# The last block of a three-layer kernel: work in halves on two engines, centred weights, and fewer small operations

## The chip, the cores and the metric

The kernel runs on one core of a Trainium2 chip. A core has a matrix engine (TensorE, "PE" in the profile, with its weight loads as "PEld"), a vector engine (VectorE, "DVE"), a scalar engine for activations (ScalarE, "ACT"), a general engine (GpSimd, "POOL") and a queue engine that issues most DMA transfers (SyncE, "SP"). Each engine works through its own list of instructions in order and waits on semaphores for the others. The metric is the device time of one execution in microseconds (us); shown is the median of several runs.

## What is computed

The input is x, (4, 128, 64, 64) in float32: 4 batches of 4096 tokens with 128 channels. Three layers follow each other, all in float32:

```python
# layer 0: attention over all tokens, 64 inner channels, no scale
q, k, v = wq @ xf, wk @ xf, wv @ xf
x = x + wo @ (softmax(k^T q) @ v)
# layer 1, attention: causal, over LayerNorm(t), scale 128**-0.5
t = t + softmax(causal(q k^T * scale)) @ v
# layer 1, recurrence
Wx = LayerNorm(t) @ W.T
Wx = (Wx - mean) * rsqrt(var + 1e-5) * gamma + beta   # mean, var over all 4*4096 tokens
y = 0
for each token: y = sigmoid(Wx[token] + y @ V.T)
t = t + ys
```

What matters here is the seam between the two parts of layer 1: the mean and variance over all tokens of `Wx` have to be complete before the first step of the recurrence, so the last block of the causal attention stands between the two.

## The kernel before, in words

`fast_path` does all of it, with the whole activation in SBUF: `xs` has 128 partitions and, for each of the 4 batches (B), 4096 columns in 8 blocks (NB) of 512 (BLK), each block being 4 pieces (TPB) of 128 tokens. An exact but slow `general_path` stands behind a flag at the end; it isn't entered for these inputs.

The attention of both layers is one list of `items`. An item is a pair of key tiles for one block of 512 queries: `scores` (lines 824 to 863) computes products into PSUM and takes their exponential on ACT, `sums` adds up denominators on DVE, `values` (885 to 923) multiplies the probabilities with the values two items later and accumulates in `acc`. When a block's last item is done, `values` copies `acc` to SBUF as `agg` (line 921 in layer 1, one ACT copy of 512 columns).

What follows for a block of layer 1 is `finish1` (721 to 800), a generator whose steps are drawn into the loop at due slots: `folded` turns the denominators (for the last block by a small product, `den_ps`, with `own` from it at line 595), `first` multiplies `agg` with the value weights (`projected`, `o_ps`, line 614), scales and adds the residual (`joined`, line 624), writes the result to DRAM and takes the LayerNorm's moments (`moments`, 629 to 640; the power -0.5 on POOL at line 638). `norm` sharpens the reciprocal root by one Newton step (`newton`, 460 to 468) and normalises four pieces on DVE (line 645). `second` transposes the normalised block; `third` multiplies it with the recurrence's weights `wf` (line 769), takes statistics on DVE (772) and copies the product to `xs` on ACT (779 or 782).

All blocks but the last transpose by DVE and DMA and lie beside other items' work. For the last block (`final`, batch 3, block 7) nothing is left to lie beside it. It transposes on PE into one PSUM tile (653), copies that on DVE (654), and `warm` fills PE with products whose result nobody reads, 9, 1 and 6 of them (line 730; two passes each).

After it, lines 1035 to 1046 make one `scale` and one `shift` per channel from the statistics of all 32 blocks: `ends` holds the aggregate of the first 31 in three columns and the last block's in six more. `rsqrt` (456 to 459) is the power on POOL and a Newton step. `shift_half` adds `v_half`, a product of V with 0.5 made early (`form_half`, 486 to 489), because the recurrence starts from 0.5.

The recurrence (1064 to 1087) doesn't walk all 4096 tokens in turn: each batch is cut into 256 chunks of 16 tokens that run side by side, each started 11 steps early. So there are 27 steps for each of 4 batches: a product with V on PE (`y_ps`, 1077), `z = Wx * scale + y_ps` on DVE (1079), and a sigmoid with `shift` as its bias on ACT (1082). The very first one (1074) takes `scale` and `shift_half` straight into the sigmoid. At the end `residual` transposes the states, adds the layer's input and writes the output.

Tile, the layer under the kernel, sets all semaphores and lays out the order of each engine's instructions by a plan of its own, program order being the priority. `tc.keep_in_program_order` pins an instruction. [...]

```python
            if not final:
                yield 1, norm
            yield 2, second
            yield 1 if final else 6 if g < 2 or g == NB - 1 else 4, third
```

Of the kernel before, what the change touches and what calls it, by code (L numbers as in the profile page):

```python
# [349 lines left out]
def fast_path(  # L350
# [98 lines left out]
    ends = const.tile([P, 9], F32, name="ends")  # L449
# [3 lines left out]
    v_half = const.tile([P, 1], F32, name="v_half")  # L453
    spare = const.tile([P, 1], F32, name="spare")

    def rsqrt(y, var, z):

        nc.gpsimd.tensor_tensor(y, var, mhalf[:, : y.shape[-1]], ALU.pow)
        newton(y, var, z)

    def newton(y, var, z, pinned=False):
        ins = nc.vector.tensor_tensor(z, y, y, ALU.mult)
        if pinned:

            tc.keep_in_program_order(ins)
        nc.vector.tensor_tensor(z, z, var, ALU.mult)
        nc.vector.tensor_scalar(z, z, -0.5, 1.5, ALU.mult, ALU.add)
        nc.vector.tensor_tensor(y, y, z, ALU.mult)

    with tc.tile_pool(name="batch", bufs=1) as batch, tc.tile_pool(name="rows", bufs=2) as rowp, tc.tile_pool(  # L470
        name="prob", bufs=4
# [6 lines left out]
        def misc(name):  # L478
            return ps_m.tile([P, BLK], F32, tag="m", name=name)
# [95 lines left out]
        def rows1(b, g):  # L575
# [3 lines left out]
            nc.scalar.copy(r, ps)  # L579
            bs[b].next.append(r)  # L580

        def folded(den, by_pe):
# [45 lines left out]
        def moments(b, g):  # L628

            st = stat.tile([P, TPB, nc.vector.BN_STATS_DIM], F32, tag="st", name="ln_st")  # L630
            mv = stat.tile([P, TPB, nc.vector.BN_AGGR_DIM], F32, tag="mv", name="ln_mv")
            for j in range(TPB):
                nc.vector.bn_stats(st[:, j], xs[:, b, ds(g * BLK + j * P, P)])  # L633
                nc.vector.bn_aggr(mv[:, j], st[:, j])
            var = stat.tile([P, TPB], F32, tag="var", name="ln_var")
            nc.vector.tensor_scalar(var, mv[:, :, 1], LN_EPS, None, ALU.add)  # L636
            y = stat.tile([P, TPB], F32, tag="rstd", name="ln_rstd")
            nc.gpsimd.tensor_tensor(y, var, mhalf, ALU.pow)  # L638
            return mv, var, y

        def normed(b, g, dst, mv, var, y, pinned=True):

            newton(y, var, stat.tile([P, TPB], F32, tag="z", name="ln_z"), pinned)
            for j in range(TPB):
                nc.vector.tensor_scalar(  # L645
                    dst[:, j], xs[:, b, ds(g * BLK + j * P, P)], mv[:, j, 0:1], y[:, j : j + 1], ALU.subtract, ALU.mult
                )

        def transposed(src, dst, name, engine):

            ps = misc(name)
            for j in range(TPB):
                nc.tensor.transpose(ps[:, ts(j, P)], src[:, j], ident)
            engine(dst, ps)
# [66 lines left out]
        def finish1(b, g):  # L721
# [4 lines left out]
            def warm(n, rhs):  # L726

                ps = ps_s.tile([P, 2 * BLK], F32, tag="s", name="warm_ps")
                for _ in range(n):
                    nc.tensor.matmul(ps[:, : BLK // 2].rearrange("p (a c) -> p a c", c=P) if len(rhs.shape) == 3 else ps[:, : BLK // 2], lhsT=ident, rhs=rhs, start=True, stop=True)  # L730

            def first():
                if final:
# [11 lines left out]
                mem["of"] = moments(b, g)  # L745

            def norm():
                normed(b, g, mem["xh"], *mem["of"], not final)
# [18 lines left out]
            def third():  # L767
                wp = misc("wx_ps")
                nc.tensor.matmul(wp, lhsT=wf, rhs=mem["xhT"], start=True, stop=True)  # L769
                if b == B - 1 and g == NB - 1:  # L770
                    in_range(True)
                nc.vector.bn_stats(ends[:, 3:] if final else stats[:, b * NB + g], wp)  # L772
                if b == B - 1 and g == NB - 2:
                    ahead()
                    in_range(False)

                to = xs[:, b, ts(g, BLK)]
                if final:
                    nc.scalar.copy(to.rearrange("p (s c) -> p s c", c=CPB), wp.rearrange("p (c s) -> p s c", s=STEPS))
                    warm(6, to[:, : BLK // 2])  # L780
                else:
                    nc.scalar.copy(  # L782
                        to.rearrange("p (s j q u) -> p s j q u", q=Q, j=TPB, s=STEPS),
                        wp.rearrange("p (q j u s) -> p s j q u", q=Q, j=TPB, s=STEPS),
                    )

            by_pe = final or g < 2

# [96 lines left out]
        def values(it):  # L885
# [24 lines left out]
            if it.last:  # L910
                if it.layer == 0:

                    if it.g == 0:
                        bt.xhT = batch.tile([P, N], F32, tag="xhT", name="xhT")
                    bt.agg = bt.xhT[:, ts(it.g, BLK)]
                    half = wk.tile([P, 2, BLK], F32, tag="half", name="half")
                    nc.scalar.copy(half, bt.acc)
                    nc.vector.tensor_tensor(bt.agg, half[:, 0], half[:, 1], ALU.add)
                else:
                    bt.agg = wk.tile([P, BLK], F32, tag="agg", name="agg")  # L920
                    nc.scalar.copy(bt.agg, bt.acc[:, 0])
# [102 lines left out]
    with tc.tile_pool(name="xr", bufs=1) as xrp, tc.tile_pool(name="y", bufs=2) as yp, tc.tile_pool(  # L1024
# [9 lines left out]

        mv = xrp.tile([P, nc.vector.BN_AGGR_DIM], F32, name="mv")
        nc.vector.bn_aggr(mv, ends)
        scale = xrp.tile([P, 1], F32, name="scale")
        var = xrp.tile([P, 1], F32, name="var")
# [7 lines left out]
        nc.vector.tensor_tensor(shift_half, shift, v_half, ALU.add)  # L1046
# [135 lines left out]
```

## Time and profile before

| what | us |
|---|---|
| median of 3 runs (lowest to highest) | 2064.52 (2064.33 to 2066.47) |
| the profiled execution, its own time | 2065.22 |
| span of its instructions | 2063.5 |
| PE busy in the span | 2046.0 |
| DVE busy | 1492.2 |
| ACT busy | 990.1 |
| POOL busy | 135.5 |
| mean granted TensorE clock | 0.999 of full speed |

The page also cuts the span into 40 equal slices of 51.6 us; each digit is an engine's busy share of a slice in tenths:

```profile
PE   9999999999999999999999999999999999999998
PEld 3333354444333345444333335544433334544456
DVE  4899867455889986644679987754588998764578
ACT  5666633323666643333466663332366664333365
POOL 1000011000000001000000001100000001100000
PEclk9999999999999999999999999999999999999999
```

PE is full in every slice but the last. The seam between attention and recurrence lies in the last slice but one, around 1974 to 1988 us, and is too short to be seen at this grain; it has to be looked up in the timeline. Durations below are those of this one execution, whose time stands 0.70 us above the median.

### The profile page before, as it was taken

Reading aid. Unit: us, or ns where it says so; the run is one execution under the profiler, and the core shown is the slowest. Engines: PE = TensorE matmul, PEld = TensorE weight load, DVE = VectorE, ACT = ScalarE, POOL = GpSimd, SP = SyncE. Lnnn points to the kernel's source line nnn. Section 1 sums busy time; section 2 is a strip of 40 time slices with the busy share of each in tenths; the row PEclk is TensorE's granted clock in tenths of the full one; section 3 lists DMA queues with packets and bytes.
Section 4 is the critical chain, followed back from the end, with each engine's and each line's share of the span. In section 5 each row is a group of like instructions: output and inputs, shape, how many; then the busy total and the mean of one; then the engine's idle time right before and its main releaser. Section 6 shows DMA issues by size and latency. Waiting matters only on the chain.

```text
span 2063.5 us, 30798 instructions
## 1 busy us (share of the span) xinstructions
PE 2046.0 (99%) x11716; PEld 896.4 (43%) x11716; DVE 1492.2 (72%) x2865; ACT 990.1 (48%) x1071; POOL 135.5 (7%) x221
## 2 busy tenths in 40 slices
PE   9999999999999999999999999999999999999998
PEld 3333354444333345444333335544433334544456
DVE  4899867455889986644679987754588998764578
ACT  5666633323666643333466663332366664333365
POOL 1000011000000001000000001100000001100000
PEclk9999999999999999999999999999999999999999
DMA  4111012220100111231011101222000111110044
GB/s 113 43 23 23 12 42 51 69 67 16 57 8 17 23 28 46 62 77 41 17 43 22 23 12 42 47 67 72 16 17 5 19 23 28 41 43 25 16 169 165
DMA packets 207148, 89.03 MB, mean 43 GB/s; under 512 B 140960, under 2 KB 189600, under 8 KB 205968
## 3 DMA queue, kind: packets, MB, share of 16 engines
q1 hardware_dynamic: 205984, 86.42, 16.4%
q8 instruction: 94, 1.54, 0.3%
q14 instruction: 62, 0.51, 0.1%
q0 software_dynamic: 288, 0.39, 0.1%
q10 hardware_dynamic: 720, 0.16, 0.0%
HBM read 45.84 MB, written 36.89 MB: 40 GB/s over the span
## 4 chain that ended last, share of the span: by engine, by line
PE 97%; DVE 1%; issue 1%; DMA 0%; ACT 0%; POOL 0%; DVEq 0%; POOLq 0%; ACTq 0%
PE s_ps L844 22%; PE acc L903 22%; PE s_ps L835 22%; PE acc L895 21%; PE o_ps L614 3%; PE y_ps L1077 2%; PE r_ps L577 1%; PE wx_ps L769 1%; PE kr_ps L520 1%; PE v_ps L532 1%; DVE xr L1098 1%; PE warm_ps L484 0%; DMA swap<-kr 0%; ACT p L849 0%; DMA out_x<-xr 0%
## 5 line engine op out<-in xcount | busy, mean ns | idle before, releaser
L875 DVE TENSOR_TENSOR dsum<-dsum,p 128x1024 f32<-128x1024 f32 x676 | 826.0, 1222 | 430.2 <-ACT p L851 312.3
L849 ACT ACTIVATE p<-s_ps,nshift 128x1024 f32<-128x1024 f32 x512 | 569.6, 1117 | 315.0 <-PE s_ps L835 304.4
L851 ACT ACTIVATE p<-s_ps 128x1024 f32<-128x1024 f32 (+2 forms) x288 | 274.5, 953 | 605.5 <-PE s_ps L844 603.2
L895 PE MATMUL acc<-p,v 64*64 64x512 f32 x4096 | 529.2, 590 | 0.0
L835 PE MATMUL s_ps<-swap,kr 64*64 64x512 f32 x2048 | 524.1, 591 | 2.5 <-ACT p L849 1.6
L835 PE MATMUL s_ps<-kr 64*64 64x512 f32 x2048 | 524.1, 591 | 0.0
L844 PE MATMUL s_ps<-rows,xhT 128*128 128x512 f32 (+3 forms) x1152 | 502.9, 559 | 0.0
L903 PE MATMUL acc<-p,xh 128*128 128x512 f32 (+3 forms) x1152 | 500.8, 557 | 0.0
L903 PEld LDWEIGHTS acc<-p,xh 128*128 128x128 f32 x1152 | 216.2, 190 | 244.3 <-issue 233.5
L844 PEld LDWEIGHTS s_ps<-rows,xhT 128*128 128x128 f32 x1152 | 213.8, 190 | 242.4 <-issue 204.6
L895 PEld LDWEIGHTS acc<-p,v 64*64 64x64 f32 x4096 | 155.5, 133 | 281.7 <-issue 269.8
L835 PEld LDWEIGHTS s_ps<-swap,kr 64*64 64x64 f32 x2048 | 139.6, 133 | 141.1 <-issue 125.2
L835 PEld LDWEIGHTS s_ps<-kr 64*64 64x64 f32 x2048 | 139.7, 133 | 138.0 <-issue 133.8
L638 POOL TENSOR_TENSOR ln_rstd<-ln_var,mhalf 128x4 f32<-128x4 f32 x64 | 89.4, 1397 | 1102.1 <-DVE ln_var L636 1102.1
L883 DVE TENSOR_TENSOR dsum<-dsum,p 128x256 f32<-128x256 f32 (+1 forms) x120 | 54.9, 493 | 66.8 <-POOL p L855 66.8
L624 DVE SCALAR_TENSOR_TENSOR xs<-o_ps,recs,xs 128x128 f32<-128x128 f32 x256 | 75.0, 341 | 3.8 <-PE o_ps L614 0.5
L645 DVE TENSOR_SCALAR xh<-xs,ln_mv,ln_rstd 128x128 f32<-128x128 f32 x256 | 71.4, 342 | 2.2
L855 POOL TENSOR_SCALAR_AFFINE_SELECT p<-p 128x128 f32<-128x128 f32 x128 | 35.4, 300 | 466.6 <-ACT p L851 451.8
L633 DVE BATCH_NORM_STATS2 ln_st<-xs 128x6 f32<-128x128 f32 x256 | 63.3, 270 | 0.0
L782 ACT COPY xs<-wx_ps 128x512 f32<-128x512 f32 x31 | 18.1, 585 | 74.6 <-DVE stats L772 68.4
L873 DVE COPY dsum<-p 128x1024 f32<-128x1024 f32 x60 | 41.0, 684 | 12.1 <-ACT p L851 7.8
L1079 DVE SCALAR_TENSOR_TENSOR z<-xs,scale,y_ps 128x256 f32<-128x256 f32 x104 | 46.8, 480 | 2.9 <-PE y_ps L1077 1.7
(138 smaller groups left out, 984.6 us busy)
## 6 DMA issues: line engine op xcount, KB each, us to landing
xs<-in_xT SPq DMA_DIRECT2D x32, 256.0 KB, 2.9
by_r<-sqT SPq DMA_DIRECT2D x128, 64.0 KB, 2.2
xhT<-by_r SPq DMA_DIRECT2D x128, 64.0 KB, 2.0
x<-xs SPq DMA_DIRECT2D x32, 256.0 KB, 2.3
xr<-x SPq DMA_DIRECT2D x8, 1024.0 KB, 12.6
out_x<-xr SPq DMA_DIRECT2D x16, 512.0 KB, 4.7
by_c<-sqT SPq DMA_DIRECT2D x124, 64.0 KB, 1.8
xhT<-by_c SPq DMA_DIRECT2D x31, 256.0 KB, 2.6
```

Of the source, the lines that this page charges most:

```text
L614: nc.tensor.matmul(op[:, ts(j, P)], lhsT=agg[:, ts(j, P)], rhs=wv1 if layer else wo2, start=True, stop=True)
L624: nc.vector.scalar_tensor_tensor(t, in0=op[:, ts(j, P)], scalar=rec[:, j : j + 1], in1=t, op0=ALU.mult, op1=ALU.add)
L633: nc.vector.bn_stats(st[:, j], xs[:, b, ds(g * BLK + j * P, P)])
L638: nc.gpsimd.tensor_tensor(y, var, mhalf, ALU.pow)
L645: nc.vector.tensor_scalar(dst[:, j], xs[:, b, ds(g * BLK + j * P, P)], mv[:, j, 0:1], y[:, j : j + 1], ALU.subtract, ALU.mult)
L835: nc.tensor.matmul(ps[c * M : c * M + M, off : off + n], lhsT=bs[it.b].kr[part, h, ds(t % (NT // 2) * P + c * M, M)], rhs=rows[h], start=True,
L844: nc.tensor.matmul(ps[:, off : off + n], lhsT=lhsT, rhs=rhs, start=True, stop=True)
L849: nc.scalar.activation(it.p[:, :off], ps[:, :off], AF.Exp, bias=nshift)
L851: nc.scalar.activation(it.p[:, :off], ps[:, :off], AF.Exp, scale=float(P) ** -0.5)
L875: nc.vector.tensor_tensor(flat, flat, it.p, ALU.add)
L895: nc.tensor.matmul(bt.acc[h * M : h * M + M, r], lhsT=bt.v[part, t % (NT // 2), t // (NT // 2)], rhs=it.p[part, o : o + n], start=it.first ...
L903: nc.tensor.matmul(bt.acc[:, 0, q0:], lhsT=bt.xh[:, t], rhs=it.p[:, o : o + n], start=it.first and h == 0, stop=it.last and h == 1,)
```

## The change

- `values`: for the very last block the copy of `acc` is cut in two, columns 0 to 255 on ACT and 256 to 511 on DVE, and `own` in `folded` is ordered behind the DVE half.
- `newton` takes `half = -0.5 * var`, made beside the power, and does three operations in place of four, the last two fused.
- `normed` for the last block: pieces 0 and 2 on DVE, 1 and 3 on ACT, multiplied by the reciprocal root only. The mean isn't subtracted; instead the last block's product uses `wfc`, weights multiplied from the left by `ident - 1/128`, made early in `form_half`.
- `second` for the last block: the four transposes go into two PSUM tiles, copied by DVE and ACT. The one warming product there is gone.
- `third` for the last block: two products of 256 columns in two tiles, with statistics on DVE and a copy on ACT for each; `ends` grows from 9 to 15 columns. Six warming products follow, now pinned to program order.
- Scale and shift: fused operations, with `beta_half` (beta plus V times 0.5) made early in place of `v_half`; `shift` comes after `shift_half`.

```diff
+    center = const.tile([P, P], F32, name="center")
+    nc.vector.tensor_scalar(center, ident, -1.0 / P, None, ALU.add)
+    wfc = const.tile([P, P], F32, name="wfc")
...
-    def newton(y, var, z, pinned=False):
+    def newton(y, half, z, pinned=False):
+
         ins = nc.vector.tensor_tensor(z, y, y, ALU.mult)
...
-        nc.vector.tensor_tensor(z, z, var, ALU.mult)
-        nc.vector.tensor_scalar(z, z, -0.5, 1.5, ALU.mult, ALU.add)
-        nc.vector.tensor_tensor(y, y, z, ALU.mult)
+        nc.vector.tensor_tensor(z, z, half, ALU.mult)
+        nc.vector.scalar_tensor_tensor(y, in0=z, scalar=1.5, in1=y, op0=ALU.add, op1=ALU.mult)
...
-            nc.vector.tensor_copy(v_half, hp[:, 0:1])
+            nc.vector.tensor_tensor(beta_half, hp[:, 0:1], beta, ALU.add)
+            cp = misc("c_ps")
+            nc.tensor.matmul(cp[:, :P], lhsT=center, rhs=wf, start=True, stop=True)
+            nc.vector.tensor_copy(wfc, cp[:, :P])
...
-                nc.vector.tensor_tensor(own, dp.rearrange("p (q j) -> p q j", q=Q), quarter, ALU.mult)
+                ins = nc.vector.tensor_tensor(own, dp.rearrange("p (q j) -> p q j", q=Q), quarter, ALU.mult)
+                if copied:
+
+                    tc.add_manual_dep(
+                        ins.ins,
+                        copied[0].ins.name,
...
+            half = stat.tile([P, TPB], F32, tag="half", name="ln_half")
+            nc.vector.tensor_scalar(half, var, -0.5, None, ALU.mult)
+            return mv, half, y
...
             for j in range(TPB):
+                if last:
+                    t = xs[:, b, ds(g * BLK + j * P, P)]
+                    if j % 2:
+                        nc.scalar.activation(dst[:, j], t, AF.Copy, scale=y[:, j : j + 1])
+                    else:
+                        nc.vector.tensor_scalar(dst[:, j], t, y[:, j : j + 1], None, ALU.mult)
+                    continue
...
                 if final:
-                    transposed(mem["xh"], mem["xhT"], "xh2T_ps", nc.vector.tensor_copy)
-                    warm(1, mem["xh"][:, 2:])
+                    for k, copy in enumerate((nc.vector.tensor_copy, nc.scalar.copy)):
+                        ps = misc("xh2T_ps")
+                        for i in range(2):
+
+                            nc.tensor.transpose(ps[:, ts(i, P)], mem["xh"][:, 2 * k + i], ident)
+                        copy(mem["xhT"][:, ts(k, BLK // 2)], ps[:, : BLK // 2])
                     return
...
+                if final:
+                    in_range(True)
+                    for k in range(2):
+                        wp = misc("wx_ps")[:, : BLK // 2]
+                        nc.tensor.matmul(wp, lhsT=wfc, rhs=mem["xhT"][:, ts(k, BLK // 2)], start=True, stop=True)
+                        nc.vector.bn_stats(ends[:, 3 + 6 * k : 9 + 6 * k], wp)
+                        nc.scalar.copy(to[:, :, ts(k, CPB // 2)], wp.rearrange("p (c s) -> p s c", s=STEPS))
+                    warm(6, xs[:, b, ds(g * BLK, BLK // 2)])
+                    return
...
-                    nc.scalar.copy(bt.agg, bt.acc[:, 0])
+                    if it.b == B - 1 and it.g == NB - 1:
+                        nc.scalar.copy(bt.agg[:, : BLK // 2], bt.acc[:, 0, : BLK // 2])
+                        copied.append(nc.vector.tensor_copy(bt.agg[:, BLK // 2 :], bt.acc[:, 0, BLK // 2 :]))
+                    else:
+                        nc.scalar.copy(bt.agg, bt.acc[:, 0])
...
-        rsqrt(scale, var, xrp.tile([P, 1], F32, name="z"))
-        nc.vector.tensor_tensor(scale, scale, gamma, ALU.mult)
-        shift = xrp.tile([P, 1], F32, name="shift")
-        nc.vector.tensor_tensor(shift, mv[:, 0:1], scale, ALU.mult)
-        nc.vector.tensor_tensor(shift, beta, shift, ALU.subtract)
-        shift_half = xrp.tile([P, 1], F32, name="shift_half")
-        nc.vector.tensor_tensor(shift_half, shift, v_half, ALU.add)
+        nc.gpsimd.tensor_tensor(y, var, mhalf[:, :1], ALU.pow)
+        nc.vector.tensor_scalar(half, var, -0.5, None, ALU.mult)
+        nc.vector.tensor_scalar(nmean, mv[:, 0:1], -1.0, None, ALU.mult)
+        nc.vector.scalar_tensor_tensor(z, in0=y, scalar=half, in1=y, op0=ALU.mult, op1=ALU.mult)
+        nc.vector.scalar_tensor_tensor(y, in0=z, scalar=1.5, in1=y, op0=ALU.add, op1=ALU.mult)
+        nc.vector.tensor_tensor(scale, y, gamma, ALU.mult)
+        nc.vector.scalar_tensor_tensor(shift_half, in0=nmean, scalar=scale, in1=beta_half, op0=ALU.mult, op1=ALU.add)
+        nc.vector.scalar_tensor_tensor(shift, in0=nmean, scalar=scale, in1=beta, op0=ALU.mult, op1=ALU.add)
```

More of the change, by code (lines that the diff above doesn't have):

```diff
@@ L447, in fast_path @@
     stats = const.tile([P, B * NB - 1, nc.vector.BN_STATS_DIM], F32, name="stats")
-    ends = const.tile([P, 9], F32, name="ends")
+    ends = const.tile([P, 15], F32, name="ends")
     nc.gpsimd.memset(ends[:, 0:1], float((B * NB - 1) * BLK))
@@ L452, in fast_path @@
     nc.gpsimd.memset(point5, 0.5)
-    v_half = const.tile([P, 1], F32, name="v_half")
+    beta_half = const.tile([P, 1], F32, name="beta_half")
     spare = const.tile([P, 1], F32, name="spare")
-    def rsqrt(y, var, z):
-        nc.gpsimd.tensor_tensor(y, var, mhalf[:, : y.shape[-1]], ALU.pow)
-        newton(y, var, z)
-    def newton(y, var, z, pinned=False):
+    def newton(y, half, z, pinned=False):
         ins = nc.vector.tensor_tensor(z, y, y, ALU.mult)
@@ L580, in rows1 @@
             bs[b].next.append(r)
+        copied = []
         def folded(den, by_pe):
@@ L594, in folded @@
                 nc.tensor.matmul(dp, lhsT=fold, rhs=part.rearrange("p q j -> p (q j)"), start=True, stop=True)
-                nc.vector.tensor_tensor(own, dp.rearrange("p (q j) -> p q j", q=Q), quarter, ALU.mult)
+                ins = nc.vector.tensor_tensor(own, dp.rearrange("p (q j) -> p q j", q=Q), quarter, ALU.mult)
[3 more added lines that the diff above has]
+                        copied[0].ins.name,
+                        mybir.DependencyInfo(mybir.DependencyClass.NoSync, mybir.DependencyReason.DATA),
+                        reason="order on DVE",
+                    )
             else:
@@ L638, in moments, with normed @@
             nc.gpsimd.tensor_tensor(y, var, mhalf, ALU.pow)
-            return mv, var, y
-        def normed(b, g, dst, mv, var, y, pinned=True):
-            newton(y, var, stat.tile([P, TPB], F32, tag="z", name="ln_z"), pinned)
-            for j in range(TPB):
+            half = stat.tile([P, TPB], F32, tag="half", name="ln_half")
+            nc.vector.tensor_scalar(half, var, -0.5, None, ALU.mult)
+            return mv, half, y
+        def normed(b, g, dst, mv, half, y, last=False):
+            newton(y, half, stat.tile([P, TPB], F32, tag="z", name="ln_z"), not last)
+            for j in range(TPB):
+                if last:
[5 more added lines that the diff above has]
+                    continue
                 nc.vector.tensor_scalar(
@@ L729, in warm @@
                 for _ in range(n):
-                    nc.tensor.matmul(ps[:, : BLK // 2].rearrange("p (a c) -> p a c", c=P) if len(rhs.shape) == 3 else ps[:, : BLK // 2], lhsT=ident, rhs=rhs, start=True, stop=True)
+                    tc.keep_in_program_order(
+                        nc.tensor.matmul(ps[:, : BLK // 2], lhsT=ident, rhs=rhs, start=True, stop=True)
+                    )
             def first():
@@ L747, in norm @@
             def norm():
-                normed(b, g, mem["xh"], *mem["of"], not final)
+                normed(b, g, mem["xh"], *mem["of"], final)
             def second():
@@ L767, in third @@
             def third():
+                to = xs[:, b, ts(g, BLK)].rearrange("p (s c) -> p s c", s=STEPS)
+                if final:
[7 more added lines that the diff above has]
+                    return
                 wp = misc("wx_ps")
                 nc.tensor.matmul(wp, lhsT=wf, rhs=mem["xhT"], start=True, stop=True)
-                if b == B - 1 and g == NB - 1:
-                    in_range(True)
-                nc.vector.bn_stats(ends[:, 3:] if final else stats[:, b * NB + g], wp)
+                nc.vector.bn_stats(stats[:, b * NB + g], wp)
                 if b == B - 1 and g == NB - 2:
@@ L775, in third @@
                     in_range(False)
[L777 to L785, printed above, removed]
+                nc.scalar.copy(
+                    to.rearrange("p s (j q u) -> p s j q u", q=Q, j=TPB),
+                    wp.rearrange("p (q j u s) -> p s j q u", q=Q, j=TPB, s=STEPS),
+                )
             by_pe = final or g < 2
@@ L1036, in fast_path @@
         nc.vector.bn_aggr(mv, ends)
-        scale = xrp.tile([P, 1], F32, name="scale")
-        var = xrp.tile([P, 1], F32, name="var")
+        one = lambda name: xrp.tile([P, 1], F32, name=name)
+        var, y, half, nmean, z = one("var"), one("y0"), one("var_half"), one("nmean"), one("z0")
+        scale, shift, shift_half = one("scale"), one("shift"), one("shift_half")
         nc.vector.tensor_scalar(var, mv[:, 1:2], BN_EPS, None, ALU.add)
-        rsqrt(scale, var, xrp.tile([P, 1], F32, name="z"))
-        nc.vector.tensor_tensor(scale, scale, gamma, ALU.mult)
-        shift = xrp.tile([P, 1], F32, name="shift")
-        nc.vector.tensor_tensor(shift, mv[:, 0:1], scale, ALU.mult)
-        nc.vector.tensor_tensor(shift, beta, shift, ALU.subtract)
-        shift_half = xrp.tile([P, 1], F32, name="shift_half")
-        nc.vector.tensor_tensor(shift_half, shift, v_half, ALU.add)
+        nc.gpsimd.tensor_tensor(y, var, mhalf[:, :1], ALU.pow)
[6 more added lines that the diff above has]
+        nc.vector.scalar_tensor_tensor(shift, in0=nmean, scalar=scale, in1=beta, op0=ALU.mult, op1=ALU.add)
         by_step = xs.rearrange("p b (g s c) -> p b s g c", s=STEPS, c=CPB)
```

## The prediction, made before the result was known

> **What bounds the kernel now.** I read first the page's chain that ended last, by engine, and then the same chain in order of time, to see where it leaves TensorE (PE).
>
> ```profile
> PE 97%; DVE 1%; issue 1%; DMA 0%; ACT 0%; POOL 0%; DVEq 0%; POOLq 0%; ACTq 0%
> ```
>
> PE makes up 97% of the end. The table by stretches gives PE 899.51 us busy of the 900 between 100 and 1000 us, and 898.89 of the next 900: nothing that another engine gains there can move the end. The loop goes on until 1973.98, and what follows is the one stretch where engines wait for each other in turn. In the chain by time (start, length, what):
>
> ```profile
> 1978.39 1.02 POOL ln_rstd L638
> ...
> 1980.23 0.35 DVE xh L645
> 1980.59 0.14 issue
> 1980.72 1.02 PE xh2T_ps L653 x4
> 1981.75 0.02 issue
> 1981.77 0.70 DVE xhT L654
> 1982.47 0.04 issue
> 1982.52 1.14 PE wx_ps L769 x2
> 1983.65 0.02 issue
> 1983.68 0.71 DVE ends L772
> 1984.39 0.02 issue
> 1984.41 0.59 ACT xs L779
> 1985.01 0.04 issue
> 1985.05 2.86 PE warm_ps L730 x12
> 1987.91 0.10 issue
> 1988.01 20.68 PE y_ps L1077 x90
> ```
>
> The reader sees a relay: one engine at a time, each handing over a whole block. The chain's last link before the recurrence is the warming matmuls; the timeline of ACT and PE says whether they really decide:
>
> ```profile
> 1974.02 0.59 ACT L921 COPY agg<-acc 128x512 f32<-128x512 f32 x1 [3.32 <-PE acc L903]
> ...
> 1984.41 0.59 ACT L779 COPY xs<-wx_ps 128x512 f32<-128x512 f32 x1 [8.29 <-DVE ends L772]
> 1987.21 2.08 ACT L1074 ACTIVATE y<-xs,shift_half,scale 128x256 f32<-128x256 f32 x4 [2.21 <-DVE shift_half L1046]
> 1989.23 10.01 ACT L1082 ACTIVATE y<-z,shift 128x256 f32<-128x256 f32 x22
> ```
>
> From 1987.21 ACT never rests (10.01/22 = 0.455 us a sigmoid, 12.00 busy of 12 in 1988 to 2000), so the recurrence is bound by ACT, and its start is bound by `shift_half`. The first y_ps (1988.01) follows the first sigmoid (ends 1987.81); warming, last issued at 1987.53, is just clear of it. After the recurrence ACT and DVE end at 2037 and the output leaves at about 400 GB/s until 2059; that tail moves as a block.
>
> So the change can act on 1974.02 to 1987.21, 13.19 us. It cannot gain the main loop.
>
> **The edits, step by step**, all against this execution.
>
> *agg in halves.* Now: ACT 0.59 us, then o_ps 1974.66 to 1975.82 (1.16 us), then L624 at 1975.85. A half on ACT is 0.39 (the 128x256 square from PSUM at L1112 took 0.384), on DVE 0.42 (between 0.284 for 128x128 at L494 and 0.692 for 128x512 at L654). [...] Row: the ACT copy L779 idled 8.29 us and left 0.03 us after DVE's statistics of the same wx_ps, though it needs nothing from them; L782 does so block after block. [...] The rows say what PE makes of that: den_ps holds PE until 1974.47 anyway, the first half is there at 1974.41, its two products (four passes at 0.125) last until 1974.98, and by then the second half is there. L653 starting at 1980.72, before the last xh, shows that PE waits by parts of a tile. So o_ps runs 1974.48 to 1975.64: **-0.18**, against +0.26 if it waited for all of agg. I take -0.18. The forced order puts `own` behind the DVE half: 1974.90 in place of 1974.51, reciprocal by 1975.50, still ahead of 1975.64; that cover is 0.14 us thick.
>
> *Newton.* Four operations at a pitch of 0.195 (1979.44 to 1980.19) become three; the new product by -0.5 runs beside the POOL power (DVE idles 1.02 us there). **-0.20**. In the other 63 blocks DVE has the same number of operations (one less, one more), under PE: 0.
>
> *Normalisation to statistics.* Counted from the first xh. Now: four at a pitch of 0.26 end at 1.12, the last transpose at 1.50, copy 1.54 to 2.23, product 2.29 to 3.41, statistics 3.45 to 4.15. After: DVE does 0 and 2, done at 0.34 and 0.60. ACT's scaled copy from SBUF is nowhere in the trace: below, 0.30 (0.202 for one column at L735 plus 127 at the copies' 0.75 ns); above, 0.43 (0.355 at the sigmoid's 1.2 ns, plus 0.077 by which L1074, with a scale, exceeds L1082). I take 0.35, near the form that also reads SBUF; pieces 1 and 3 end at 0.38 and 0.68. Transposes 0.38 later, as now: 0.76 and 1.06. Copies: DVE 0.80 to 1.22, ACT 1.10 to 1.49, in different buffers. First product at 1.28; now it takes 1.12, less one pass's difference of 0.43: until about 1.98. The second follows on PE, until 2.41. Statistics of 256 columns are 0.41 (0.268 for 128, 0.700 for 512): 2.02 to 2.43 and 2.45 to 2.86. 4.15 - 2.86: **-1.29**. The removed mean costs nothing, since the centred weights take it out; the removed warming pair stood behind the transposes, beside DVE's copy.
>
> *Scale and shift.* Eight operations from the power to `shift_half` become four (z, y, scale, shift_half); the two factors -0.5 and -1 hide under POOL's 0.55, `shift` goes behind. A fused operation on 128x1 is not in the trace; the products there are 0.159, and I take the same pitch of 0.195: **-0.78**. Aggregating 15 columns in place of 9: +0.02.
>
> The first sigmoid: 1987.21 - 0.18 - 0.20 - 1.29 - 0.78 + 0.02 = **1984.78**. ACT waited 0.24 between `shift_half` and that sigmoid; I keep it, it may shrink to 0.03.
>
> *What is late next: warming.* Its operand needs both copies of wx, and the second copy follows the second statistics: 2.90 to 3.29 after the first xh, which is now at 1979.85, so 1983.14. Warming starts at 1983.19 and issues its last pass 2.48 later, 1985.67; y_ps gets PE at 1985.88, while its sigmoid is done at 1985.38. The first z's sigmoid stood 1.22 after y_ps: 1987.10. ACT alone would be ready at 1984.78 + 2.02 = 1986.80. The later counts: 1989.23 becomes 1987.10, **-2.13**; warming takes 0.30 of what the small operations gained.
>
> *Centred weights.* `center` (0.23 on DVE) falls into DVE's 4.54 us of idling before 8.66. The c_ps product is PE work in the full loop: two passes of 0.107 plus the change of shape, 0.21 to 0.32 (g_ps and h_ps together took 0.53). It is the third tile in a pool of two buffers: placed straight behind h_ps it would wait for g's copy, at 39.54, with all of PE behind it: 1.4 more. I take **+0.30**, ends 0.21 and 1.7. `beta_half` now waits for beta too, issued at 6.38 and landed 6.6 later, long before 39.
>
> Sum: -2.13 + 0.30 = -1.83. The profiled execution was 2065.22 (span 2063.5 and 1.7 around it), so 2063.4; the median shown is 2064.52, 0.7 below it, and the same gain gives **2062.7**. About 0.2% (4.1 us) is what a measurement of this kernel can tell from no change: by my sum the kernel is faster by 0.09%, and that counts as within.
>
> **Rivals.**
> 1. *The third tile stalls PE at 38 us.* For it: DVE took g only at 39.26, behind a 1.23 us sum. Against: the instructions are laid out by a planner that knows the buffers and has score products ready to go first. -2.13 + 1.7 = -0.4: 2064.1. Chance 0.12.
> 2. *The halves don't run beside each other*: ACT's first scaled copy waits long or takes 0.6, and o_ps waits for all of agg. Then normalisation gains nothing (+0.44) and agg costs 0.26 in place of -0.18: -0.95, 2063.6. Chance 0.06.
> 3. *Slower: the TensorE clock falls at the start of the recurrence*, since the pair of warming passes is gone and the block is thin in PE work. At half clock y_ps takes 0.86 in place of ACT's 0.455, so 0.47 us are lost in each us of it; above 1.83/0.47 = 3.9 us of half clock the kernel is slower than before. Six us: 2065.5. For: the granted clock falls to 0.50 at the end, when PE has long stopped. Against: it does so only in 2058 to 2059, over 4 us after the last matmul at 2054.3; gaps of 1.4 and 1.0 us now leave it at 1.00, and I find none above 1.1 afterwards. Chance 0.05, mostly within 0.2%.
> 4. *The tail is laid out otherwise.* All instructions are planned anew. DVE's residual adds (0.68 each) all stand behind 2036.5 now, and the output, 20 us of DMA, starts at 2038. DVE has 1.8 us idle in 1988 to 2036 by the stretches; adds moved in there would start the output 2 to 3 us earlier: 2060.2. For: five transposes for it already stand inside the recurrence. Against: nothing in that part of the text changes. Chance 0.15.
>
> The forecast itself has 0.62. Its own range: the unknown costs above come to about 0.7 each way, 2062.0 to 2063.5. For 8 in 10 I go to rival 1 above and most of the way to rival 4 below: 2060.9 to 2064.3. Faster by over 0.2% (below 2060.4) is rival 4 and little else, 0.16; slower by as much only the far end of rival 3, 0.03; within, 0.81.
>
> **What would show it.** Right: ACT's second wx copy starting just after the second statistics; the first sigmoid about 10.8 us after the agg copy starts (13.19 now); y_ps directly behind the last warming pass; one more pair of passes near 38 us and PE full otherwise; the recurrence unchanged at 0.455. Wrong: a gap on PE near 38 to 40 us, a table load on ACT before the scaled copies, a granted clock under 1.00 after 1984, residual adds before the last z, or o_ps starting only after DVE's half.

## The result, and the profile after

| | before | after |
|---|---|---|
| median of 20 runs each (lowest to highest), us | 2065.07 (2064.02 to 2067.81) | 2062.44 (2061.74 to 2062.69) |
| ratio, 95% interval | | 0.9984 (0.9978 to 0.9991) |
| span of the profiled execution, us | 2063.5 | 2060.7 |

The forecast was 2062.7. It was met in part by luck: the seam gained most of what was forecast for it, but two effects of 2.30 and 1.48 us that the sum did not have stand against each other. The times of the kernel before lie in two groups, up to about 2065.7 and from about 2066 on (9 of these 20); the upper one is told of below (the clock), and the profiled execution of before belongs to the lower. One run of the kernel before, of the 52 beside the first experiments below, was slow, at 5606.84 us, and is left out of all comparisons.

The changed kernel's chain of waits by time (start, length, what), at the same place as before:

```profile
1978.84 0.30 DVE xh L664
1979.14 0.14 issue
1979.28 0.42 PE xh2T_ps L780 x2
1979.70 0.02 issue
1979.72 0.44 DVE xhT L781
1980.16 0.04 issue
1980.20 0.71 PE wx_ps L801 x2
1980.91 0.02 issue
1980.94 0.44 DVE ends L802
1981.38 0.03 ACTq L803
1981.41 0.04 issue
1981.45 0.37 ACT xs L803
1981.82 0.02 issue
1981.84 0.38 ACT xs L803
1982.22 0.04 issue
1982.26 2.86 PE warm_ps L752 x12
1985.12 0.10 issue
1985.22 9.96 PE y_ps L1113 x43
```

Each link is now shorter, most of them by a third or more, and the chain runs through ACT's two copies and the warming into y_ps. What the warming costs is seen in ACT's timeline:

```profile
1973.04 0.37 ACT L952 COPY agg<-acc 128x256 f32<-128x256 f32 x1 [3.33 <-PE acc L933]
...
1983.94 2.07 ACT L1110 ACTIVATE y<-xs,shift_half,scale 128x256 f32<-128x256 f32 x4 [1.73 <-DVE shift L1082]
1986.45 3.62 ACT L1118 ACTIVATE y<-z,shift 128x256 f32<-128x256 f32 x8 [0.44 <-DVE z L1115]
```

Before the first sigmoid with z, ACT idles 0.44; in the kernel before it had no such gap. From agg to that sigmoid it is now 13.41 us (1973.04 to 1986.45), before 15.21 (1974.02 to 1989.23): the seam gains 1.80. But the spans differ by 2.8. Following the exponentials of both traces, which are the same in number and order, shows where else the time went:

| stretch | after against before, us |
|---|---|
| first exponential (at 15.12 before, 14.66 after) | -0.46 |
| the early product near 38 us | +1.78 |
| handover from each batch to the next (at 542, 1034, 1525) | -0.72, -0.72, -0.86 |
| seam | -1.80 |
| recurrence and tail | 0.00 |
| sum | -2.78 |

The first line is chance: in the profiles of this study the first exponential lies anywhere from 13.86 to 15.43, and one and the same kernel (one tile and four warming products, below), profiled twice, had 15.11 and 13.86. In most of the profiles the first score product waits there for the early DMA of `swap` (0.92 us in the kernel before).

**The early product.** The changed kernel's timeline at 38 us:

```profile
37.77 1.07 PE L865 MATMUL s_ps<-swap,kr 64*64 64x512 f32 x2
38.80 0.28 DVE L496 COPY g<-g_ps 128x128 f32<-128x128 f32 x1
39.00 0.15 DVE L488 TENSOR_TENSOR beta_half<-h_ps,beta 128x1 f32<-128x1 f32 x1
39.14 0.30 PEld L490 LDWEIGHTS c_ps<-wf,center 128*128 128x128 f32 x2 [1.18 <-DVE g L496]
39.14 0.49 PE L490 MATMUL c_ps<-wf,center 128*128 128x128 f32 x2 [0.30 <-DVE beta_half L488]
...
40.70 1.11 ACT L879 ACTIVATE p<-s_ps,nshift 128x1024 f32<-128x1024 f32 x1 [3.07 <-PE s_ps L865]
```

and the same exponential in the kernel before:

```profile
39.39 1.11 ACT L849 ACTIVATE p<-s_ps,nshift 128x1024 f32<-128x1024 f32 x1 [1.30 <-PE s_ps L835]
```

c_ps stands behind a single score product (two passes in the first row, 1.07 us; in the kernel before it runs side by side with three others, all eight passes within 0.91, and here the three come only after c_ps) and waits for DVE, which empties the tiles of g and h one after the other. ACT waits 3.07 us for its next scores, against 1.30 before: the difference is the 1.78 of the table, to the last digit's rounding.

**The handovers.** In the kernel before, around the first of them (DVE, POOL, ACT, PE, each from its own timeline):

```profile
525.76 1.22 DVE L875 TENSOR_TENSOR dsum<-dsum,p 128x1024 f32<-128x1024 f32 x1
525.93 1.91 POOL L638 TENSOR_TENSOR ln_rstd<-ln_var,mhalf 128x4 f32<-128x4 f32 x1 [16.69 <-DVE ln_var L636]
527.88 0.16 DVE L462 TENSOR_TENSOR ln_z<-ln_rstd 128x4 f32<-128x4 f32 x1 [0.90 <-POOL ln_rstd L638]
...
540.87 0.69 DVE L772 BATCH_NORM_STATS2 stats<-wx_ps 128x6 f32<-128x512 f32 x1
541.59 0.59 ACT L782 COPY xs<-wx_ps 128x512 f32<-128x512 f32 x1 [3.16 <-DVE stats L772]
542.08 2.13 ACT L849 ACTIVATE p<-s_ps,nshift 128x1024 f32<-128x1024 f32 x2
...
543.25 0.65 PE L835 MATMUL s_ps<-swap,kr 64*64 64x512 f32 x2 [0.49 <-ACT p L849]
```

and in the changed kernel:

```profile
527.21 0.17 DVE L652 TENSOR_SCALAR ln_half<-ln_var 128x4 f32<-128x4 f32 x1
527.26 1.01 POOL L650 TENSOR_TENSOR ln_rstd<-ln_var,mhalf 128x4 f32<-128x4 f32 x1 [16.70 <-DVE ln_var L648]
527.29 1.25 DVE L905 TENSOR_TENSOR dsum<-dsum,p 128x1024 f32<-128x1024 f32 x1
528.46 0.15 DVE L462 TENSOR_TENSOR ln_z<-ln_rstd 128x4 f32<-128x4 f32 x1
...
541.23 0.69 DVE L808 BATCH_NORM_STATS2 stats<-wx_ps 128x6 f32<-128x512 f32 x1
541.96 0.58 ACT L812 COPY xs<-wx_ps 128x512 f32<-128x512 f32 x1 [2.21 <-DVE stats L808]
542.44 2.12 ACT L879 ACTIVATE p<-s_ps,nshift 128x1024 f32<-128x1024 f32 x2
```

Before, DVE starts its 1.22 us sum right behind ln_var, and POOL's power, started 0.17 later, takes 1.91; DVE then idles 0.90 for it. Now the small product by -0.5 stands between the two: the power starts first, takes 1.01, and DVE goes on without a gap. With the shorter Newton step DVE is 0.96 ahead. (Here the loop of the changed kernel as a whole stands 1.32 later by the clock, the early product's 1.78 less the start-up's 0.46; that has to be taken off to compare the lines.) DVE then works off eight sums back to back (10.49 us in both kernels), the statistics of the previous batch's last product come 0.96 sooner, ACT's copy that waits for them lets the exponentials behind it go, and PE never runs dry. Before, PE stood for 0.49 at 543.25, and the eight score passes behind that gap took 1.09 in place of 0.86: that is the handover's 0.72. Over the whole kernel 29 of the 64 powers took over 1.3 us before, and 6 after. The power that starts behind a sum is the long one (1.91 against 1.01). The other way round shows next to nothing: the sum that starts 0.03 behind the power takes 1.25 against 1.22. The traces show who waits, not what for.

### The profile page after: what moved, and what is told of

The parts are those of the page before. It is cut to its first block, busy times and chain, and to the rows that moved or that the text cites. A ratio compares the mean times of both kernels' runs of the same rounds, so it can differ in the third digit from the quotient of the medians.

```text
span 2060.7 us, 30809 instructions
## 1 busy us (share of the span) xinstructions
PE 2046.4 (99%) x11718; PEld 913.8 (44%) x11718; DVE 1491.3 (72%) x2866; ACT 990.4 (48%) x1075; POOL 114.9 (6%) x221
## 4 chain that ended last, share of the span: by engine, by line
PE 98%; DVE 1%; issue 1%; DMA 0%; POOL 0%; ACT 0%; DVEq 0%; POOLq 0%; ACTq 0%
PE s_ps L874 22%; PE acc L933 22%; PE s_ps L865 22%; PE acc L925 21%; PE o_ps L626 3%; PE y_ps L1113 2%; PE r_ps L579 1%; PE kr_ps L522 1%; PE wx_ps L807 1%; PE v_ps L534 1%; DVE xr L1134 1%; PE warm_ps L483 0%; DMA out_x<-xr 0%; PE warm_ps L752 0%; PE vT_ps L559 0%
## 5 line engine op out<-in xcount | busy, mean ns | idle before, releaser
L925 PE MATMUL acc<-p,v 64*64 64x512 f32 x4096 | 542.1, 590 | 0.0
L865 PE MATMUL s_ps<-swap,kr 64*64 64x512 f32 x2048 | 537.6, 591 | 0.0
L925 PEld LDWEIGHTS acc<-p,v 64*64 64x64 f32 x4096 | 165.4, 133 | 273.3 <-issue 252.8
L865 PEld LDWEIGHTS s_ps<-swap,kr 64*64 64x64 f32 x2048 | 149.8, 133 | 130.1 <-issue 109.0
L650 POOL TENSOR_TENSOR ln_rstd<-ln_var,mhalf 128x4 f32<-128x4 f32 x64 | 68.2, 1065 | 1104.4 <-DVE ln_var L648 1104.4
```

Source lines behind the costliest of these rows:

```text
L865: nc.tensor.matmul(ps[c * M : c * M + M, off : off + n], lhsT=bs[it.b].kr[part, h, ds(t % (NT // 2) * P + c * M, M)], rhs=rows[h], start=True,
L925: nc.tensor.matmul(bt.acc[h * M : h * M + M, r], lhsT=bt.v[part, t % (NT // 2), t // (NT // 2)], rhs=it.p[part, o : o + n], start=it.first ...
```

## The experiments

Times are medians in us; in brackets stands the median of the kernel before, measured anew at the same time. "z" is the way from agg to the first sigmoid with z (after: 13.41), "sigmoid" that to the first sigmoid (10.90).

**One tiny DVE operation alone.** The kernel before, plus:

```diff
             nc.gpsimd.tensor_tensor(y, var, mhalf, ALU.pow)
+            half = stat.tile([P, TPB], F32, tag="half", name="ln_half")
+            nc.vector.tensor_scalar(half, var, -0.5, None, ALU.mult)
             return mv, var, y
```

> The kernel before, with one more DVE operation of 128x4 (0.17 us) behind ln_var in every block; its result is not used. Theory (POOL's power gets started before DVE's next sum): the powers over 1.3 us fall from 29 of 64 to fewer than 10, the PE gaps at the three batch handovers (0.49, 0.49, 0.62 us) vanish, and the attention ends 2.3 us earlier; the seam keeps its length of 13.2 us. Time about 2.3 below before. Rival (the gaps vanished because the whole program was laid out anew, or because of the early product for the centred weights): the gaps stay, the time is that of before or slightly longer.

Measured 2062.80 (before 2066.35), ratio 0.9989 (0.9980 to 0.9998). The handovers gain 0.72, 0.72 and 0.85 us: 2.29 together, PE gaps gone; 11 of 64 powers stay long, where fewer than 10 were expected. Both medians mix two groups; the lower ones alone (7 of the 12 runs, and 23 of before) have medians of 2062.31 and 2064.43, 2.12 apart. An operation whose result nobody reads, 0.17 us on DVE in each of 64 blocks, makes the kernel faster: the theory that the order of start matters holds. The profile caught something else. Its seam took 17.82 to z, not 15.21, and its table by stretches (length; busy PE, PEld, DVE, ACT, POOL; granted clock; DMA share and GB/s) shows why:

```profile
1978.00:1980.00 2.00, 1.65 (x6) 0.80 (x6) 1.01 (x3) 0.00 (x0) 0.00 (x0) 0.96 0.00 0
1980.00:1982.00 2.00, 1.23 (x2) 0.00 (x0) 0.73 (x2) 0.00 (x0) 0.11 (x1) 0.50 0.00 0
1982.00:1984.00 2.00, 1.36 (x3) 1.18 (x4) 1.15 (x8) 0.59 (x1) 0.55 (x1) 0.50 0.71 229
1984.00:1986.00 2.00, 2.00 (x6) 1.56 (x5) 0.48 (x3) 1.19 (x3) 0.00 (x0) 0.50 1.00 410
1986.00:1988.00 2.00, 1.90 (x7) 1.29 (x7) 0.00 (x0) 0.88 (x2) 0.00 (x0) 0.83 0.99 418
```

The granted clock is 0.50 for some 6.8 us of the seam, from 1979.8 on, and the twelve warming passes last 4.83 in place of 2.86. But for the tiny operation this seam is that of the kernel before.

**The old Newton step in the changed kernel** (no `half`, four operations):

```diff
-        nc.vector.scalar_tensor_tensor(y, in0=z, scalar=1.5, in1=y, op0=ALU.add, op1=ALU.mult)
+        nc.vector.tensor_scalar(z, z, -0.5, 1.5, ALU.mult, ALU.add)
+        nc.vector.tensor_tensor(y, y, z, ALU.mult)
...
-            half = stat.tile([P, TPB], F32, tag="half", name="ln_half")
-            nc.vector.tensor_scalar(half, var, -0.5, None, ALU.mult)
-            return mv, half, y
+            return mv, var, y
```

> The changed kernel with the Newton step of the blocks as it was: four operations, no -0.5 product beside the power. Theory: about 29 of 64 powers over 1.3 us again, PE gaps at the three handovers again, attention 2.3 us longer, and the seam 0.2 us longer: some 2.5 us above the changed kernel. Rival (the rewritten third step or the early product removed the gaps): no gaps, only the 0.2 us.

Measured 2064.66 (before 2066.35). 29 long powers, PE gaps of 0.49 at each handover; the handovers lose 2.17 of the 2.30 us again, and z is 13.61, 0.20 longer. The mirror image: the theory holds, and neither the rewritten `third` nor the early product removes the gaps.

**Both early products in one PSUM tile**, in the changed kernel:

```diff
             nc.tensor.matmul(hp[:, 0:1], lhsT=vf, rhs=point5, start=True, stop=True)
+            nc.tensor.matmul(hp[:, P : 2 * P], lhsT=center, rhs=wf, start=True, stop=True)
             nc.vector.tensor_tensor(beta_half, hp[:, 0:1], beta, ALU.add)
-            cp = misc("c_ps")
-            nc.tensor.matmul(cp[:, :P], lhsT=center, rhs=wf, start=True, stop=True)
-            nc.vector.tensor_copy(wfc, cp[:, :P])
+            nc.vector.tensor_copy(wfc, hp[:, P : 2 * P])
```

> The changed kernel with h_ps and the centred-weights product in one PSUM tile, side by side. Theory (the 1.78 us near 38 us are the wait for g's buffer, 0.46, a score product running without its three companions, 0.91, and the product itself, 0.42): the wait and the lone product go, 0.2 to 0.4 stays; the time falls by about 1.4. Rival (the loss is the added work and the change of shape): less than 0.4 falls away.

Measured 2060.99 (before 2066.35), ratio 0.9978 (0.9971 to 0.9985). The step at 38 us falls from 1.78 to 0.33:

```profile
37.87 0.47 PE L488 MATMUL h_ps<-wf,center 128*128 128x128 f32 x2
38.27 0.65 PE L864 MATMUL s_ps<-swap,kr 64*64 64x512 f32 x2
38.28 0.65 PE L864 MATMUL s_ps<-kr 64*64 64x512 f32 x2
```

No wait, and the score products stay together. The product itself costs 0.33; the third tile cost 1.45. How the 1.45 divides into the wait and the parted score products is read from one trace; no run holds the two apart.

**Four warming products in place of six**, `warm(4, ...)` in the changed kernel.

> The changed kernel with 4 in place of 6 warming products ahead of the recurrence. Theory (the last warming pass delays y_ps): y_ps comes right after its sigmoid, ACT's 0.44 us of idling before the first sigmoid with z goes, the recurrence starts 0.44 earlier and the time falls by 0.44. Rival (y_ps is held by the row of semaphore waits behind the warming, not by its length): nothing falls. Rival (the clock needs six): the granted clock falls under 1.00 in the recurrence and the time grows by a microsecond or more.

Measured 2061.91 (before 2066.35); z 12.88, 0.53 shorter, ACT without a gap, y_ps 0.05 behind its sigmoid's end. Warming was on the path. The granted clock of its profile is 1.00 up to 2054, and no run left the 1.2 us between 2061.27 and 2062.44.

**Transposes, copy, product and statistics whole again**, with the one warming product behind the transposes, as before:

```diff
+                    transposed(mem["xh"], mem["xhT"], "xh2T_ps", nc.vector.tensor_copy)
+                    warm(1, mem["xh"][:, 2:].rearrange("p j c -> p (j c)"))
...
-                    for k in range(2):
-                        wp = misc("wx_ps")[:, : BLK // 2]
-                        nc.tensor.matmul(wp, lhsT=wfc, rhs=mem["xhT"][:, ts(k, BLK // 2)], start=True, stop=True)
-                        nc.vector.bn_stats(ends[:, 3 + 6 * k : 9 + 6 * k], wp)
-                        nc.scalar.copy(to[:, :, ts(k, CPB // 2)], wp.rearrange("p (c s) -> p s c", s=STEPS))
+                    wp = misc("wx_ps")
+                    nc.tensor.matmul(wp, lhsT=wfc, rhs=mem["xhT"], start=True, stop=True)
+                    nc.vector.bn_stats(ends[:, 3:], wp)
+                    nc.scalar.copy(to, wp.rearrange("p (c s) -> p s c", s=STEPS))
```

> The changed kernel with transposes, copy, product and statistics of the last block whole again, as before; everything else stays. Theory on the path: normalisation keeps its 0.4, the halves' 0.8 to 0.9 goes, and the warming starts later by as much: the recurrence starts about 1.0 later. Theory on the clock (the seam before was thin enough in PE work, gaps of 1.02, 0.35 and 1.41, for the clock to fall to half in about half of the executions, at some 2.5 us each): the times spread over more than 2 us again, some near 2063.4 and some near 2065.5, with lower mean clocks in the latter. Rival (the spread of before comes from elsewhere, for example the four-product start or DMA): a spread under 1 us as in the changed kernel.

Measured 2063.88 (before 2065.45). Sigmoid 11.64 (0.74 later), z 14.43 (1.02 later): the path as expected. The clock isn't: none of 20 runs (2063.23 to 2064.83, all with mean clocks of 0.998 or 0.999) is in an upper group. So the halves aren't what keeps the clock up.

**The eight small operations again**, in the changed kernel:

```diff
-        nc.vector.scalar_tensor_tensor(z, in0=y, scalar=half, in1=y, op0=ALU.mult, op1=ALU.mult)
-        nc.vector.scalar_tensor_tensor(y, in0=z, scalar=1.5, in1=y, op0=ALU.add, op1=ALU.mult)
+        nc.vector.tensor_tensor(z, y, y, ALU.mult)
+        nc.vector.tensor_tensor(z, z, var, ALU.mult)
+        nc.vector.tensor_scalar(z, z, -0.5, 1.5, ALU.mult, ALU.add)
+        nc.vector.tensor_tensor(y, y, z, ALU.mult)
...
+        nc.vector.tensor_tensor(shift_half, shift, half, ALU.add)
```

> The changed kernel with the eight dependent small operations for scale and shift of before. Theory (warming covers part of the chain): the first sigmoid comes 0.78 later after agg, 11.7 in place of 10.9, but the first sigmoid with z only about 0.35 later, 13.8 in place of 13.4, and the time grows by 0.35. Rival (the chain is on the path in full): both 0.78.

Measured 2062.88 (before 2065.45). Sigmoid 11.68, 0.78 later; z 13.66, 0.25 later. Two thirds of what the fused operations gain is covered by the warming. One of its 19 runs stands apart, at 2065.10; the others lie between 2062.35 and 2063.61.

**agg copied whole:**

```diff
-                    if it.b == B - 1 and it.g == NB - 1:
-                        nc.scalar.copy(bt.agg[:, : BLK // 2], bt.acc[:, 0, : BLK // 2])
-                        copied.append(nc.vector.tensor_copy(bt.agg[:, BLK // 2 :], bt.acc[:, 0, BLK // 2 :]))
-                    else:
-                        nc.scalar.copy(bt.agg, bt.acc[:, 0])
+                    nc.scalar.copy(bt.agg, bt.acc[:, 0])
```

> The changed kernel with acc of the last block copied whole on ACT. Theory (the halves run one after the other on one bank, but PE starts on the first): the residual join starts 0.2 later, and so does all that follows. Rival (halves in series on one bank lose 0.26): it starts earlier or at the same place.

Measured 2063.13 (before 2065.45). The residual join starts 1.83 after agg (1973.81 to 1975.64), against 1.63 in the changed kernel; z 13.61. The split is worth 0.20, although its halves don't overlap: in the changed kernel DVE's half starts at 1973.44, behind ACT's, which ends at 1973.41, and o_ps starts at 1973.46 without waiting for it.

**One tile and four warming products together.**

> The changed kernel with h_ps and the centred-weights product in one tile and four warming products. Theory: both gains add, 1.4 and 0.5, for about 2060.5, 1.9 below the changed kernel and below every kernel so far, with a spread of 1 us. Rival (the clock needs more warming, or the program is laid out anew): the spread grows or one of the two gains is lost.

Measured 2060.98 (before 2065.45), ratio 0.9974 (0.9963 to 0.9984). z is 12.89 and the step at 38 us 0.33: both gains are there in the trace, but the median is that of one tile alone (2060.99, measured at another time) and doesn't show the second. So the two were measured side by side:

> The changed kernel with one tile for the two early products, again, beside the next one. Theory: 2061.0.

> One tile and four warming products ahead of the recurrence, beside the run before. Theory: the 0.53 us that the traces show between the two at the first sigmoid with z is seen in the medians too, 2060.5. Rival: the medians are the same, since the spread of the start-up covers it.

Measured 2061.03 and 2060.19 (before 2064.90), ratios 0.9978 (0.9969 to 0.9988) and 0.9973 (0.9962 to 0.9984). The two together are the best kernel of the study, some 2 us below the changed one (1.96 by the traces, counted from the first exponential). The intervals of the two ratios overlap, since both carry the spread of the kernel before; directly, its 7 runs (2059.67 to 2060.68) lie below the 10 of one tile alone (2060.67 to 2061.55), but for one pair. The medians differ by 0.84; the traces give 0.53 of it to the path (z 13.41 and 12.88).

**The clock, from both sides.** The kernel before with `warm(11, agg[:, : BLK // 2])` in place of 9:

> The kernel before with 11 in place of 9 warming products behind the last block's o_ps (0.86 us more PE work where PE idles 1.02). Theory (the upper group of before's times, at 2066 and above in about half of the executions, is the clock falling to half because PE is too thinly used between the warming and the recurrence, idle 2.78 us in three gaps; the changed kernel idles 1.96 there): idle falls to 1.9, the upper group vanishes, all times lie between 2063.9 and 2065.7, the seam keeps its 13.2 us. Rival (the upper group has another cause): about half of the times stay above 2066.

and the changed kernel with `warm(5, agg[:, : BLK // 2])`:

> The changed kernel with 5 in place of 9 warming products behind o_ps; nothing on the path. Theory: PE idle in the three gaps grows from 1.96 to about 3.7, the clock falls to half in a part of the executions, those are about 2 us longer and show a lower mean clock, the others stay at 2062.4. Rival: all stay at 2062.4.

The first: 2064.85 (before 2064.90). The first gap shrank to 0.16 and the seam kept its 13.2 to the sigmoid, but 3 of 12 times are still above 2066.6; 16 of 40 were in the upper group in the kernel before beside it. That is no clear difference, and the expectation that the upper group vanishes was wrong. The second: 2064.85 in the median, 2062.48 to 2066.74; 14 of 20 times are at 2064.3 or above, all with mean clocks of 0.997 or less, the others at 2063.6 or below with 0.998 and more. Its profiled execution shows the path unchanged (z 13.41) at a granted clock of 1.00. So taking eight warming passes from the changed kernel's seam brings an upper group back; what keeps it away in the changed kernel is only partly known. The falling clock itself was seen in the seam of one trace, that of the tiny operation. For the upper group of the kernel before it is inferred: those runs have mean clocks of 0.997 or 0.998 (one 0.999), the others 0.998 or 0.999, and none of them was profiled.

## Why the prediction was right, point by point

- **agg in halves**: forecast -0.18, measured -0.20; serial halves, and PE starting on the first, as worked out. No run shows the +0.26 that was set against it, for o_ps waiting for both halves: these ended 0.82 after agg's start, and o_ps started 0.42 after it. ACT's half took 0.372 against the 0.39 assumed.
- **Newton**: -0.20, measured -0.21 on the path. "In the other 63 blocks ... under PE: 0" was **wrong**. The count of operations was right, but not what their order does: 2.30 us, shown by the tiny operation alone (2.29) and by the old Newton step (2.17 lost). With it falls "It cannot gain the main loop". The sign stood in the prediction's own table: PE lacks 0.49 us of being full between 100 and 1000 us and 1.11 in the next 900, and these are the three gaps at the handovers, 0.49, 0.49 and 0.62.
- **Normalisation to statistics**: -1.29, measured -1.19 (4.15 to 2.96). ACT's scaled copy took 0.394, inside the bounds of 0.30 and 0.43, and statistics of 256 columns 0.432 against 0.41.
- **Scale and shift**: -0.76 with the longer aggregation, measured -0.69 (2.83 to 2.14 from the statistics' end). The fused operations with a scalar from SBUF took 0.22, not 0.16. ACT started 0.16 behind `shift_half` (0.24 before); the profile puts its release to `shift`, one operation later, which the sigmoid doesn't read.
- **Warming**: cover of 0.30 forecast, 0.49 measured. Its start was right (9.22 after agg, 9.17 forecast). The mistake was to let y_ps follow the last warming pass after 0.21; it follows after 0.48, at 12.18. The kernel before had shown it: there too y_ps came 0.48 behind the last warming pass (1987.53 to 1988.01) and 0.20 behind its sigmoid, where 0.05 is enough with four warming products. So warming was not "just clear": it already held y_ps up by 0.15, which ACT's four sigmoids in a row hid.
- **Seam in all**: -2.13 forecast, -1.80 measured.
- **Centred weights**: +0.30 forecast, +1.78 measured. What I gave 0.12 as rival 1 is what happened: the planner put c_ps early and PE waited. By the trace the wait was shorter than the 1.4 I priced (0.46), but a score product ran without its three companions for the 0.91 that all four take together in the kernel before; the product alone, in one tile, costs 0.33.
- **Tail and recurrence**: unchanged, rival 4 didn't occur.
- **Rival 3** had the clock right and the kernel wrong. It is the kernel before whose times, by the mean clocks, show a falling clock in a good part of its executions (28 of 51, 24 of 59, 16 of 40 in the upper group), and all 20 runs of the changed one stay below 2062.7. Against the lower group alone, about 2064.6, the change is worth some 2.2 us.

The steps that failed are thus "the new product by -0.5 runs beside the POOL power", taken to cost or gain nothing in the other blocks (0 forecast, -2.30 measured), and with the opposite sign the placing of c_ps (+0.30 forecast, +1.78 measured). Their errors, -2.30 and +1.48, and the seam's +0.33 leave -0.49, which with the start-up's -0.46 is the difference between the forecast's -1.83 and the traces' -2.78. That the forecast lay 0.3 us from the median is luck in two ways: the errors cancel in part, and -1.83 was set off from 2064.52, a median of three runs that is close to the lower group's.

## What to carry to other kernels

Where GpSimd has a short operation on the way and DVE has a long sum ready, see to it that GpSimd starts first: one tiny DVE operation between the two was worth 2.3 us here. A new product in a full matmul loop can cost more than its own time (1.78 against 0.33 here): give it room in a tile that is there, and look whether it parts products that run side by side. When a path is shortened, look at filler work that seemed harmless: six warming products became the last link, and four did as well. And when an engine is full for 899.51 us of 900, ask what the rest is before calling the loop closed.

## What the runs showed of the hardware

- In the kernel before, 24 of POOL's powers (128x4) started 0.08 to 0.18 us after one of DVE's 128x1024 sums, and every one ended 0.86 to 0.87 after that sum did, having taken 1.91 to 2.01. In the changed kernel 20 of them started 0.03 before such a sum: each took 1.01, and the sum 1.24 to 1.25 in place of 1.22. So in these traces the sum holds the power up, and the power hardly holds the sum up. The one power that started only 0.02 ahead of a sum before took 2.14, and the one 0.01 ahead in the changed kernel 2.15.
- The granted clock fell to 0.50 at 1979.8 in the run with the tiny operation, behind PE gaps of 1.02 and 0.35; the gap of 1.41 came after the fall. The changed kernel with whole products, with gaps of 0.76, 0.35 and 1.45, showed no upper group in 20 runs, and the kernel before with eleven warming products, with 0.16, 0.35 and 1.41, did in 3 of 12. What brings the fall on, these runs don't settle.
- PE's idle time alone does not decide it: from 1976 to 1980 PE was busy for 2.63 us with the tiny operation, and the granted clock fell; in the profile with five warming products it was busy for 1.47 us there, and the clock stayed at 1.00 up to 1990. Why executions of one kernel differ in this, no run shows.
- The first y_ps comes 0.48 behind the issue of the last warming pass in both kernels, its sigmoid being ready by then, while warming passes follow each other by 0.216. A change of operands alone doesn't explain it: the first warming pass follows the last o_ps pass by 0.11. What else y_ps waits for wasn't tested.
